# Six more block pairs of y in half products, Wv loaded behind them, and the residual of layer 0 on ScalarE and by an adding gather

## The chip, the cores and the metric

The kernel runs on one core of a Trainium2 chip, in fp32. The metric is device time in microseconds (us) of one launch, as the median of several runs. One further execution was taken with the hardware profiler; its views (busy times, windows, waits, timelines, the chain that ended last) are what this document argues from. TensorE is called PE in the views, VectorE DVE, ScalarE ACT, GpSimd POOL and the SyncE queue SP.

## The reference

Two layers on N = 2708 rows of D = 1024, over one sparse adjacency matrix. Cut to what matters:

```python
# layer 0
q = x @ Wq.T + bq;  k = x @ Wk.T + bk;  v = x @ Wv.T + bv
z = (q @ k.T) / sqrt(1024) * adj
z = where(z == 0, -10000, z)
x1 = layernorm(x + relu(softmax(z) @ v))
# layer 1
out = layernorm(x1 + adj @ (x1 @ W) + b)
```

## The kernel before, in words

**Blocks.** The rows are sorted by their number of neighbours and cut into 22 blocks of 128 (the last has 20). For a block, only the rows of x that its neighbours name are gathered.

**Algebra.** The scores q·k need only y = x·M with M = Wq·Wk (and some constants): a score is the dot product of a row of y with a row of x. Since softmax weights sum to one, the weighted sum is taken over rows of x first and projected by Wv afterwards. So layer 0 is: M, y for all blocks, scores, softmax and weighted row sums per block (`attend`), then a projection by Wv, relu, the residual and the layer norm.

**Stages.** From 0 to about 131 us TensorE makes M while VectorE lists the adjacency's columns. From 131 to 245 us it makes y for blocks 0 to 7, two blocks at a time, by `pair_products` (L334): Strassen-Winograd's scheme with seven half products of 8 passes (one pass is a 128x128 weight load and a 128x512 matmul) where two plain blocks take eight. From 245 to about 428 us it makes y for blocks 8 to 20, one after another, by `y_block` (L383, 32 passes), and the 20 rows of block 21 by `y_last` (L445). Then come ten projection pairs, again by `pair_products`, to about 745 us, and layer 1 to the end.

**pair_products.** It needs the four block sums S0 to S3 of the rows (made by GpSimd in `y_sums_of`, L402, for y; by VectorE for the projection) and three weight differences t2 to t4. Its three PSUM banks pa, pb and pc (`bank`, L321: four buffers in all) are used again inside the pair: product 3 (S1·t2) goes on in the bank of product 1, after its copy to SBUF; product 5 (S2·t3) in that of 3, after its copy; product 6 in that of 4, after its copy; product 7 in that of 5, after an add. The copies are `nc.scalar.copy` when there is no base to add (y), and VectorE adds when there is (the projection's bias); both are in `add` (L327, the instruction at L330 or L332). There are four ScalarE copies and three or more VectorE adds per pair of y.

**y_block.** A plain block fills two accumulators of 16 passes each; every third block takes its two banks from the transposes' pool (`spare_bank`, L324; "tr" in the views). ScalarE copies both to `yo` and SP stores it.

**Order of the work.** Each engine takes its instructions in the order in which the program was scheduled. The attention of the blocks is cut into jobs; a list of steps (y blocks, then projection pairs) hands them out by a credit: each step adds a planned time (`COST`, `STEP`, `PAIR`, ...) and each job takes its own off, so the constants decide how many jobs come between two steps. A job gathers rows (GpSimd, `gather_slot`, L482, and `gather_onto`, L472, where ScalarE first copies a row and the gather adds to it), takes dot products (VectorE, L1020), a softmax (ScalarE, L1058), and weighted sums (ScalarE L1077 for the first, VectorE L1079 for the others). ScalarE also sums x's columns (`column_sums`, L458, eight instructions a block).

**finish_pair** (L1214). After a projection, per half of a block, VectorE takes relu of t and adds the row of x, which GpSimd gathered ahead into a buffer (L1220, with the row sum as a by-product); then `norm` (ScalarE L982 and L995 with small VectorE steps) and a scatter of x1 (L926).

**Buffers.** Gathered rows go into G1 = 9 buffers, used in turn, in layer 1 too. Wv (16 loads of 256 KB) is loaded piecewise during y; the differences t3 and t4 of y's weights have a pool of their own.

Of the kernel before, what the change touches and what calls it, by code (L numbers as in the profile page):

```python
# [9 lines left out]
F32 = mybir.dt.float32  # L10
# [4 lines left out]
U8 = mybir.dt.uint8  # L15
# [26 lines left out]
EARLY = 13  # L42
G1 = 9
RB = 5
# [39 lines left out]
def sparse_part(ctx, tc, x, xT, adj, wqT, wkT, wvT, bq, bk, bv, w1, b1, out):  # L84
# [28 lines left out]
    with es:  # L113
# [219 lines left out]

        def pair_products(A, S, w, ts, base, to, whole, first_alone=False):  # L334
# [26 lines left out]
            add(to[0][1], pa, base[0][1])  # L361
            half_products(pc, S[0], t1, stop=False)
            add(to[1][1], pc, base[1][1])
            half_products(pa, S[2], t3, start=False, stop=False)
            whole(1, 1, pa, to[1][1])
            half_products(pc, S[3], w22, start=False)
            whole(0, 1, pc, to[0][1])
            products.append(half_products(pa, a22, t4, start=False))
            whole(1, 0, pa, base[1][0])
# [13 lines left out]
        def y_block(b):  # L383
            yo = yos[b % 3]
            to = halves_of(yo)
            firsts = []
            for h in range(NH):
                po = spare_bank() if b % 3 == 1 else bank()
                for c in range(DC):
                    put = nc.tensor.matmul(po, xts[b][:, c, :], m_q[c // 4][h][:, c % 4], start=(c == 0), stop=(c == DC - 1))  # L390
                    if c % (DC // 2) == 0:
                        firsts.append(put)
                add(to[h], po, None)
            products.append(put)
            if b != NB - 2:
                column_sums(b, firsts)
            if b == NB - 4:
                column_sums(NB - 2, [put] * (DC // 2))
            load_x()
            y_store(b, yo)  # L400

        def y_sums_of(b):  # L402
            (a11, a12), (a21, a22) = [halves_of_turned(x_) for x_ in xts[b:b + 2]]
            S = [y_sums[b // 2 % 2][:, i] for i in range(4)]
            nc.gpsimd.tensor_tensor(S[0], a21, a22, op=ALU.add)
            nc.gpsimd.tensor_tensor(S[1], S[0], a11, op=ALU.subtract)
            nc.gpsimd.tensor_tensor(S[3], a12, S[1], op=ALU.subtract)
            nc.gpsimd.tensor_tensor(S[2], a11, a21, op=ALU.subtract)

        def y_pair(b):  # L410
            yo = [yos[(b + k) % 3] for k in range(2)]
            to, base = [halves_of(t) for t in yo], [[None] * NH] * 2
            left = [NH, NH]

            def whole(k, h, acc, what):
                add(to[k][h], acc, what)
                left[k] -= 1
                if not left[k]:
                    load_x()
                    y_store(b + k, yo[k])  # L420

            at = len(began)
            pair_products(xts[b:b + 2], [y_sums[b // 2 % 2][:, i] for i in range(4)], y_w, y_t, base, to, whole)
            firsts = began[at:]
            for k in range(2):
                column_sums(b + k, firsts[3 * k:3 * k + 4])
            if b + 2 < FAMILY:
                y_sums_of(b + 2)
# [28 lines left out]

        def column_sums(b, behind=None):  # L458
            xt = xts[b] if b < NB - 1 else x_last
            for c in range(DC):  # L460
                put = nc.scalar.activation(junka[:, :xt.shape[2]], xt[:, c, :], AF.Copy, accum_out=xs[:, c, b:b + 1])  # L461
                if behind is not None and c % 2 == 0:
                    follow(put, behind[c // 2])
# [40 lines left out]
        def deal_hub():  # L504
# [71 lines left out]
            nc.tensor.matmul(mm[:, P:P + 1], ones, more, start=True, stop=True)  # L576
            place = small("place", P)
            nc.vector.tensor_copy(place, mm[:, :P])
# [231 lines left out]
        wb.release()  # L810
        yb = tc.alloc_tile_pool(name="yb", bufs=1, reuse_waits="tile")
        y_sums = []
        y_sums.append(yb.tile([P, 4, DC // 2, P], F32, name="y_s0"))
        t3 = yb.tile([P, DC // 2, HALF], F32, name="y_t3")
        t4 = yb.tile([P, DC // 2, HALF], F32, name="y_t4")
        y_sums.append(yb.tile([P, 4, DC // 2, P], F32, name="y_s1"))
# [4 lines left out]
        junka = xa.tile([P, P], F32, name="junka", bufs=1)  # L821
        x_last = xa.tile([P, DC, HUB], F32, name="x_last", bufs=1)
        nc.vector.memset(x_last, 0.0)
        xts = []
# [16 lines left out]

        def load_wv(cs):
            for c in cs:
                for h in range(NH):
                    put = nc.sync.dma_start(out=wv_q[c // 4][h][:, c % 4, :], in_=wvT[c * P:(c + 1) * P, h * HALF:(h + 1) * HALF])
                    follow(put, products[-2])

        wv_q = [None, quarters_of("wv", (1,))[0]]
        while counted[0] < done:
            count_columns(began[-1])  # L850
        for b in range(0, FAMILY, 2):
# [23 lines left out]
            if b in (0, 2, 6):  # L875
                next(deal)
            if b >= 4:
                load_wv(range(DC // 2 + b - 4, DC // 2 + b - 2))
        later_records = sort_end(1, products[-1])
        wv_q[0] = quarters_of("wv", (0,))[0]  # L880
        yb.release()
        la.release()
# [331 lines left out]
        def finish_pair(pair, ts):  # L1214
            for k, (b, t) in enumerate(zip(pair, ts)):
                ends = half_stats() if k and pair == pairs[-1] else None
                xr, sums = pair_x[b], [stat.tile([P, 1], F32, name=f"sm{h}", bufs=6) for h in range(NH)]
# [11 lines left out]

        STEP, Y_END, PAIR, EVICT, FLIP, END, SLOT, SMALL = 14.2, 4.8, 24.3, 7.5, 2.2, 3.3, 2.6, 1.5  # L1230
        got, xb_bc, xb_pools, pair_x = {}, [], [], {}
# [8 lines left out]
        steps += [("p", pairs[0]), ("mean", tuple(last))] + [("p", pair) for pair in pairs[1:]]  # L1240
        COST = {"p": PAIR - EVICT + FLIP, "mean": 5.6, NB - 1: 2.0}

# [94 lines left out]

        credit = 0
        turned = {}
# [9 lines left out]

        for i, (kind, b) in enumerate(steps):  # L1350
# [4 lines left out]
            credit += COST.get(kind, COST.get(b, STEP - Y_END))  # L1355
            step[0] = i
            join(i, 3 if left_y else 1)
            if kind == "y" and b == NB - 3:
                (q11, q12), (q21, q22) = wv_q
                follow(nc.vector.tensor_sub(q12, q12, q11), products[-2])  # L1360
            if kind == "p" and b == pairs[0]:

                wv_t = differences()
# [16 lines left out]
            if kind == "y":  # L1380
# [9 lines left out]
                if 3 <= b - FAMILY < 7:  # L1390
                    load_wv([b - FAMILY - 3])
                if b == FAMILY + 1:
                    column_sums(NB - 1)
                left_y -= 1
# [464 lines left out]
```

## Time and profile before

| what | us |
|---|---|
| median of three runs | 1039.84 |
| lowest, highest run | 1035.62, 1050.41 |
| the profiled execution's own time | 1041.33 |
| its span | 1039.6 |
| TensorE, VectorE, ScalarE, GpSimd busy | 966.2, 834.8, 424.5, 581.6 |
| mean granted TensorE clock | 0.971 of full |

In the lines below, a row of the waits is: engine, line and tile that waited, what it waited for, total us, times, longest us. A row of a timeline is: start, us, engine, line, operation, tiles and shapes, and in brackets the idle time before it with what ended it. A row of the groups is: line, engine, operation, tiles, count | busy us, mean ns of one | idle before. A row of the windows is: window, its length, then busy us (and instructions) of PE, PEld (weight loads), DVE, ACT and POOL, the granted clock, the DMA share and GB/s.

### The profile page before, as it was taken

Reading aid. Unit: us, or ns where it says so; the run is one execution under the profiler, and the core shown is the slowest. Engines: PE = TensorE matmul, PEld = TensorE weight load, DVE = VectorE, ACT = ScalarE, POOL = GpSimd, SP = SyncE. Lnnn points to the kernel's source line nnn. Section 1 sums busy time; section 2 is a strip of 40 time slices with the busy share of each in tenths; the row PEclk is TensorE's granted clock in tenths of the full one; section 3 lists DMA queues with packets and bytes.
Section 4 is the critical chain, followed back from the end, with each engine's and each line's share of the span. In section 5 each row is a group of like instructions: output and inputs, shape, how many; then the busy total and the mean of one; then the engine's idle time right before and its main releaser. Section 6 shows DMA issues by size and latency. Waiting matters only on the chain.

```text
span 1039.6 us, 10519 instructions
## 1 busy us (share of the span) xinstructions
PE 966.2 (93%) x2723; PEld 456.3 (44%) x2723; DVE 834.8 (80%) x2017; ACT 424.5 (41%) x932; POOL 581.6 (56%) x455
## 2 busy tenths in 40 slices
PE   7989987899999999897999999997899999989994
PEld 6434433344444444444544444443444444534441
DVE  8999997963768863999999999986569877869632
ACT  4634474554534434134343545322322333352721
POOL 3841044432666742456857776681678888868410
PEclk9989998999999999898999999998999999989997
DMA  9455896677889863345837888898598699987631
GB/s 353 150 185 172 240 288 188 191 251 192 211 257 316 274 199 113 120 125 153 247 109 214 265 237 248 270 277 318 173 306 215 218 298 309 310 261 220 186 116 44
DMA packets 103069, 229.23 MB, mean 220 GB/s; under 512 B 19678, under 2 KB 47078, under 8 KB 103000
## 3 DMA queue, kind: packets, MB, share of 16 engines
q0 software_dynamic: 51152, 159.06, 50.8%
q1 hardware_dynamic: 51848, 69.41, 20.8%
q8 instruction: 23, 0.38, 0.1%
q14 instruction: 46, 0.38, 0.1%
HBM read 218.10 MB, written 33.64 MB: 242 GB/s over the span
## 4 chain that ended last, share of the span: by engine, by line
PE 43%; DVE 24%; DMA 14%; issue 11%; POOL 5%; ACT 2%; SPq 0%; POOLq 0%; DVEq 0%; ACTq 0%
PE po L310 24%; PE po L390 11%; DVE at_a L239 6%; PE tr L390 5%; DMA g<-x_d,tabs 3%; POOL g L482 3%; DVE r L1455 2%; DVE junkv L1020 2%; DVE r L1079 1%; DMA xr<-x_d,tabs 1%; DMA yg<-y_d,tabs 1%; POOL xr L466 1%; DMA g<-in_x_dram,tabs 1%; DMA g<-x_d,tab_h 1%; DMA g<-in_x_dram,rec_h 1%
## 5 line engine op out<-in xcount | busy, mean ns | idle before, releaser
L310 PE MATMUL po<-t,s_all 128*128 128x512 f32 x320 | 146.5, 600 | 5.3 <-DVE xr L332 4.8
L482 POOL DMA_INDIRECT g<-in_x_dram,tabs x84 | 117.4, 1398 | 56.3 <-issue 14.6
L390 PE MATMUL po<-m,xt 128*128 128x512 f32 x288 | 124.8, 592 | 0.0
L1455 DVE SCALAR_TENSOR_TENSOR r<-g,valid,r 128x1024 f32<-128x1024 f32 x77 | 98.1, 1280 | 13.8 <-DMA g<-x_d,tabs 10.8
L1020 DVE SCALAR_TENSOR_TENSOR junkv<-yg,g 128x1024 uint8<-128x1024 f32 x84 | 102.4, 1219 | 4.4 <-DMA yg<-y_d,tabs 2.7
L310 PEld LDWEIGHTS po<-t,s_all 128*128 128x128 f32 x320 | 60.7, 192 | 83.3 <-issue 70.7
L482 POOL DMA_INDIRECT g<-x_d,tabs x66 | 78.3, 1186 | 23.2 <-issue 14.6
L1079 DVE SCALAR_TENSOR_TENSOR r<-g,pr,r 128x1024 f32<-128x1024 f32 x64 | 81.8, 1279 | 6.4 <-ACT r L1077 5.8
L390 PEld LDWEIGHTS po<-m,xt 128*128 128x128 f32 x288 | 54.6, 190 | 68.2 <-issue 67.7
L982 ACT ACTIVATE junks<-t,lnm 128x1024 uint8<-128x1024 f32 (+1 forms) x40 | 45.9, 1147 | 93.6 <-DVE lnm L980 93.5
L239 DVE FIND_INDEX8 at_a<-ones,a 128x8 uint16<-128x83 f32 (+3 forms) x132 | 82.0, 627 | 0.0
L310 PE MATMUL po<-wv,s_all 128*128 128x512 f32 x160 | 74.5, 610 | 8.0 <-DVE t L332 6.4
L310 PE MATMUL po<-w,rT 128*128 128x512 f32 x160 | 75.2, 612 | 4.4 <-DVE t L1492 4.2
L461 ACT ACTIVATE junka<-xt 128x128 f32<-128x128 f32 x168 | 51.8, 308 | 61.1 <-PE po L310 28.2
L255 ACT ACTIVATE junk<-a 128x2756 uint8<-128x2756 uint32 (+1 forms) x22 | 55.0, 2501 | 49.7 <-issue 31.6
L310 PE MATMUL po<-t,rT 128*128 128x512 f32 x160 | 74.4, 608 | 0.7 <-DVE t L332 0.7
L940 ACT COPY rT<-tr 128x512 f32<-128x512 f32 x76 | 41.3, 588 | 81.2 <-PE tr L939 81.1
L310 PE MATMUL po<-wv,rT 128*128 128x512 f32 x160 | 73.9, 613 | 0.0
L310 PE MATMUL po<-w,s_all 128*128 128x512 f32 x160 | 72.4, 593 | 0.7 <-DVE xr L332 0.7
L995 ACT ACTIVATE t<-t,nmr,rstd 128x1024 f32<-128x1024 f32 (+1 forms) x40 | 48.8, 1237 | 42.7 <-DVE nmr L994 38.2
L390 PE MATMUL tr<-m,xt 128*128 128x512 f32 x128 | 55.6, 592 | 0.0
L926 POOL DMA_INDIRECT x_d<-t,tabs x22 | 27.2, 1236 | 45.8 <-ACT t L995 35.1
(415 smaller groups left out, 1818.1 us busy)
## 6 DMA issues: line engine op xcount, KB each, us to landing
xt<-in_xT_dram SPq DMA_DIRECT2D x21, 512.0 KB, 8.9
y_d<-yo SPq DMA_DIRECT2D x21, 512.0 KB, 6.8
a<-in_adj_dram SPq DMA_DIRECT2D x21, 413.5 KB, 5.9
a<-in_adj_dram SPq DMA_DIRECT2D x21, 338.5 KB, 5.1
a<-in_adj_dram SPq DMA_DIRECT2D x21, 263.5 KB, 3.3
wq_i<-in_wqT_dram SPq DMA_DIRECT2D x8, 512.0 KB, 7.0
wk_i<-in_wkT_dram SPq DMA_DIRECT2D x8, 512.0 KB, 10.2
wv<-in_wvT_dram SPq DMA_DIRECT2D x16, 256.0 KB, 10.0
```

Source lines behind the costliest of these rows:

```text
L239: nc.vector.max_index(at[:n, i], ones[:n, :8], a[:n, cuts[i] + 8 * i:cuts[i + 1] + 8 * i + 8])
L255: put = nc.scalar.activation(junk[:n], loaded[b][:n, :AW].bitcast(U32), AF.Sign, accum_out=cnt[:n, b:b + 1])
L310: put = nc.tensor.matmul(acc, a[:, k], w[:, k], start=start and k == 0, stop=stop and k == DC // 2 - 1, skip_group_check=True)
L390: put = nc.tensor.matmul(po, xts[b][:, c, :], m_q[c // 4][h][:, c % 4], start=(c == 0), stop=(c == DC - 1))
L461: put = nc.scalar.activation(junka[:, :xt.shape[2]], xt[:, c, :], AF.Copy, accum_out=xs[:, c, b:b + 1])
L482: nc.gpsimd.indirect_dma_start(out=dst[:n], out_offset=None, in_=src, in_offset=bass.IndirectOffsetOnAxis(ap=at, axis=0), bounds_check=N - ...
L940: nc.scalar.copy(rT[:, g * 4:g * 4 + 4, :], tr)
L982: nc.scalar.activation(junks[:n], t[:n], AF.Square, bias=nm[:n], accum_out=vs[:n])
L995: applied.append(nc.scalar.activation(t[:n], t[:n], AF.Identity, bias=nmr[:n], scale=rstd[:n]))
L1020: put = nc.vector.scalar_tensor_tensor(junkv[:n], yg[:n], scale, xg[:n], op0=ALU.mult, op1=ALU.mult, accum_out=s)
L1079: nc.vector.scalar_tensor_tensor(r[:n], xg[j][:n], pr[:n, j:j + 1], r[:n], op0=ALU.mult, op1=ALU.add)
L1455: put = nc.vector.scalar_tensor_tensor(r[:n], xg[:n], ok[:n, j:j + 1], r[:n], op0=ALU.mult, op1=ALU.add)
```

## The change

**Pairs.** Blocks 8 to 19 of y are made as six pairs by `y_pair` instead of twelve plain blocks; block 20 stays plain, after block 21. The jobs of the second block of a pair are now placed behind product 4 (`halfway`). The block sums have one buffer each instead of two, and S2 is written over the first half of the second block's own rows; x's column sums of these columns are put right by a scale of 2 in the first block and −1 in the second. Plain blocks no longer use the transposes' banks.

**Wv.** t3 and t4 live in two of Wv's slots, and Wv is loaded whole behind the last pair.

**finish_pair.** For all projection pairs but the last, ScalarE takes relu of t in place, GpSimd gathers x's rows onto t by adding, and ScalarE takes the sum by a pass of its own. No buffer of x's rows is gathered ahead for these pairs.

**Constants.** G1 is 8 instead of 9; a half of a pair is planned at 8.9 us, and the end of a block at 2.0 instead of 3.3.

```diff
-G1 = 9
+G1 = 8
...
-            half_products(pc, S[0], t1, stop=False)
+            put = half_products(pc, S[0], t1, stop=False)
+            if halfway is not None:
+                products.append(put)
+                halfway()
...
         def y_sums_of(b):
             (a11, a12), (a21, a22) = [halves_of_turned(x_) for x_ in xts[b:b + 2]]
-            S = [y_sums[b // 2 % 2][:, i] for i in range(4)]
-            nc.gpsimd.tensor_tensor(S[0], a21, a22, op=ALU.add)
-            nc.gpsimd.tensor_tensor(S[1], S[0], a11, op=ALU.subtract)
-            nc.gpsimd.tensor_tensor(S[3], a12, S[1], op=ALU.subtract)
-            nc.gpsimd.tensor_tensor(S[2], a11, a21, op=ALU.subtract)
+            s0, s1, s3 = y_sums
+            nc.gpsimd.tensor_tensor(s0, a21, a22, op=ALU.add)
+            nc.gpsimd.tensor_tensor(s1, s0, a11, op=ALU.subtract)
+            nc.gpsimd.tensor_tensor(a21, a11, a21, op=ALU.subtract)
+            nc.gpsimd.tensor_tensor(s3, a12, s1, op=ALU.subtract)
...
+            def halfway():
+                column_sums(b, began[at:at + 4], 2.0)
+                load_x()
+                if ahead is not None:
+                    ahead()
+
+            s0, s1, s3 = y_sums
+            pair_products(xt, [s0, s1, xt[1][:, :DC // 2], s3], y_w, y_t, base, to, whole, halfway=halfway)
+            column_sums(b + 1, began[at + 3:at + 7], -1.0)
+            if b + 3 < NB - 1:
                 y_sums_of(b + 2)
...
+        t3, t4 = [wv_pool.tile([P, DC // 2, HALF], F32, name=f"y_t{k}", tag=f"v{k - 1}") for k in (3, 4)]
...
         def finish_pair(pair, ts):
             for k, (b, t) in enumerate(zip(pair, ts)):
-                ends = half_stats() if k and pair == pairs[-1] else None
+                if pair != pairs[-1]:
+                    nc.scalar.activation(t, t, AF.Relu)
+                    gather_at(x, tabs[:, b, ROW:ROW + 1], P, t, ALU.add)
+                    sm = stat.tile([P, 1], F32, name="sm")
+                    nc.scalar.activation(junks, t, AF.Copy, accum_out=sm)
+                    norm(t, sm, P)
+                    scatter(x1_d[:, :], b, P, t, "x1")
+                    continue
+                ends = half_stats() if k else None
...
-        STEP, Y_END, PAIR, EVICT, FLIP, END, SLOT, SMALL = 14.2, 4.8, 24.3, 7.5, 2.2, 3.3, 2.6, 1.5
+        STEP, Y_END, HALF_PAIR, PAIR, EVICT, FLIP, END, SLOT, SMALL = 14.2, 4.8, 8.9, 24.3, 7.5, 2.2, 2.0, 2.6, 1.5
...
-                (y_last if b == NB - 1 else y_block)(b)
...
+        for i, (kind, b) in enumerate(steps):
+            if kind != "y" or b >= NB - 2 or b % 2 == 0:
+                ahead(i)
+            if kind == "y":
+                if b < NB - 2:
+                    if b % 2 == 0:
+                        y_pair(b, lambda: ahead(i + 1))
...
+                        if b == NB - 4:
+                            column_sums(NB - 2, [products[-1]] * (DC // 2))
+                            wv_q = quarters_of("wv")
+                            load_wv()
+                else:
+                    (y_last if b == NB - 1 else y_block)(b)
...
-                for k, b_ in enumerate(b):
+                for k, b_ in enumerate(b if b == pairs[-1] else ()):
                     pair_x[b_] = gather_x(x, b_, k)
```

More of the change, by code (lines that the diff above doesn't have):

```diff
@@ L332, in add, with pair_products @@
                     nc.vector.tensor_add(to, acc, what)
-        def pair_products(A, S, w, ts, base, to, whole, first_alone=False):
+        def pair_products(A, S, w, ts, base, to, whole, first_alone=False, halfway=None):
             (w11, t1), (w21, w22) = w
@@ L385, in y_block @@
             to = halves_of(yo)
-            firsts = []
             for h in range(NH):
-                po = spare_bank() if b % 3 == 1 else bank()
+                po = bank()
                 for c in range(DC):
                     put = nc.tensor.matmul(po, xts[b][:, c, :], m_q[c // 4][h][:, c % 4], start=(c == 0), stop=(c == DC - 1))
-                    if c % (DC // 2) == 0:
-                        firsts.append(put)
                 add(to[h], po, None)
             products.append(put)
[L395 to L399, printed above, removed]
             y_store(b, yo)
@@ L403, in y_sums_of, with y_pair @@
             (a11, a12), (a21, a22) = [halves_of_turned(x_) for x_ in xts[b:b + 2]]
-            S = [y_sums[b // 2 % 2][:, i] for i in range(4)]
-            nc.gpsimd.tensor_tensor(S[0], a21, a22, op=ALU.add)
-            nc.gpsimd.tensor_tensor(S[1], S[0], a11, op=ALU.subtract)
-            nc.gpsimd.tensor_tensor(S[3], a12, S[1], op=ALU.subtract)
-            nc.gpsimd.tensor_tensor(S[2], a11, a21, op=ALU.subtract)
-        def y_pair(b):
+            s0, s1, s3 = y_sums
[3 more added lines that the diff above has]
+            nc.gpsimd.tensor_tensor(s3, a12, s1, op=ALU.subtract)
+        def y_pair(b, ahead=None):
             yo = [yos[(b + k) % 3] for k in range(2)]
@@ L418, in whole @@
                 if not left[k]:
-                    load_x()
+                    if k:
+                        load_x()
                     y_store(b + k, yo[k])
             at = len(began)
[L423 to L427, printed above, removed]
+            xt = xts[b:b + 2]
+            def halfway():
+                column_sums(b, began[at:at + 4], 2.0)
+                load_x()
+                if ahead is not None:
[4 more added lines that the diff above has]
+            if b + 3 < NB - 1:
                 y_sums_of(b + 2)
@@ L456, in y_last, with column_sums @@
                 nc.sync.dma_start(out=y_ds[1][o0:o0 + n, cs], in_=yo[gs, cs])
-        def column_sums(b, behind=None):
+        def column_sums(b, behind=None, of_first=1.0):
             xt = xts[b] if b < NB - 1 else x_last
             for c in range(DC):
-                put = nc.scalar.activation(junka[:, :xt.shape[2]], xt[:, c, :], AF.Copy, accum_out=xs[:, c, b:b + 1])
+                put = nc.scalar.activation(junka[:, :xt.shape[2]], xt[:, c, :], AF.Copy, scale=of_first if c < DC // 2 else 1.0,
+                                           accum_out=xs[:, c, b:b + 1])
                 if behind is not None and c % 2 == 0:
@@ L576, in deal_hub @@
             nc.tensor.matmul(mm[:, P:P + 1], ones, more, start=True, stop=True)
-            place = small("place", P)
+            place = alike
             nc.vector.tensor_copy(place, mm[:, :P])
@@ L810, in sparse_part @@
         wb.release()
[L811 to L816, printed above, removed]
+        t3, t4 = [wv_pool.tile([P, DC // 2, HALF], F32, name=f"y_t{k}", tag=f"v{k - 1}") for k in (3, 4)]
         nc.vector.tensor_sub(t3, t2, m_q[0][0])
@@ L820, in sparse_part @@
         xs = xa.tile([P, DC, NB], F32, name="xs", bufs=1)
-        junka = xa.tile([P, P], F32, name="junka", bufs=1)
+        junka = xa.tile([P, P], U8, name="junka", bufs=1)
         x_last = xa.tile([P, DC, HUB], F32, name="x_last", bufs=1)
+        y_sums = [xa.tile([P, DC // 2, P], F32, name=f"y_s{i}", bufs=1) for i in (0, 1, 3)]
         nc.vector.memset(x_last, 0.0)
@@ L840, in sparse_part, with load_wv @@
         deal = deal_hub()
[L842 to L848, printed above, removed]
+        def load_wv():
+            for i in range(2):
+                for j in range(2):
+                    for c in range(DC // 2):
+                        nc.sync.dma_start(out=wv_q[i][j][:, c, :],
+                                          in_=wvT[(i * DC // 2 + c) * P:(i * DC // 2 + c + 1) * P, j * HALF:(j + 1) * HALF])
         while counted[0] < done:
@@ L876, in sparse_part @@
                 next(deal)
-            if b >= 4:
-                load_wv(range(DC // 2 + b - 4, DC // 2 + b - 2))
         later_records = sort_end(1, products[-1])
-        wv_q[0] = quarters_of("wv", (0,))[0]
-        yb.release()
         la.release()
@@ L1240, in sparse_part @@
         steps += [("p", pairs[0]), ("mean", tuple(last))] + [("p", pair) for pair in pairs[1:]]
-        COST = {"p": PAIR - EVICT + FLIP, "mean": 5.6, NB - 1: 2.0}
+        COST = {"p": PAIR - EVICT + FLIP, "mean": 5.6, NB - 1: 2.0, NB - 2: STEP - Y_END}
         def blocks_of(step):
@@ L1336, in raise_flag @@
             nc.vector.tensor_scalar(flag, mm[:1, 0, :1], 0.0, None, op0=ALU.is_gt)
-        credit = 0
+        credit, wv_q = 0, None
         turned = {}
@@ L1348, in turn, with ahead @@
                             ring.remove(b_)
-        for i, (kind, b) in enumerate(steps):
+        def ahead(i):
+            nonlocal credit, pending, wv_t
+            kind, b = steps[i]
             for p in pending:
@@ L1354, in sparse_part @@
             pending = []
-            credit += COST.get(kind, COST.get(b, STEP - Y_END))
+            credit += COST.get(kind, COST.get(b, HALF_PAIR))
             step[0] = i
             join(i, 3 if left_y else 1)
-            if kind == "y" and b == NB - 3:
+            if kind == "y" and b == NB - 2:
                 (q11, q12), (q21, q22) = wv_q
@@ L1361, in sparse_part @@
             if kind == "p" and b == pairs[0]:
+                (q11, q12), (q21, q22) = wv_q
                 wv_t = differences()
@@ L1388, in sparse_part @@
                     nc.sync.dma_start(out=bias_bc, in_=bv.to_broadcast([P, D]))
-                (y_last if b == NB - 1 else y_block)(b)
[L1390 to L1393, printed above, removed]
+        wv_t = None
+        for i, (kind, b) in enumerate(steps):
[5 more added lines that the diff above has]
+                        y_pair(b, lambda: ahead(i + 1))
+                        if b == FAMILY:
+                            column_sums(NB - 1)
+                        if b == NB - 4:
[4 more added lines that the diff above has]
+                    (y_last if b == NB - 1 else y_block)(b)
                 left_y -= 1
```

## The prediction

> **What bounds the kernel now.** I read the page's busy times and chain first.
>
> ```profile
> PE 966.2 (93%) x2723; PEld 456.3 (44%) x2723; DVE 834.8 (80%) x2017; ACT 424.5 (41%) x932; POOL 581.6 (56%) x455
> PE 43%; DVE 24%; DMA 14%; issue 11%; POOL 5%; ACT 2%; SPq 0%; POOLq 0%; DVEq 0%; ACTq 0%
> ```
>
> TensorE leads and VectorE follows, but an average over stages says little. So next the busy time in the windows of the stages that the change touches (columns: window, length, then each engine's busy us).
>
> ```profile
> 165.00:245.00 80.00, 76.48 (x191) 34.68 (x190) 56.75 (x225) 42.62 (x124) 26.07 (x26) 1.00 0.67 213
> 245.00:413.00 168.00, 168.00 (x449) 74.62 (x448) 110.43 (x195) 75.73 (x287) 94.97 (x72) 1.00 0.77 227
> 540.00:600.00 60.00, 59.58 (x163) 27.85 (x162) 59.83 (x135) 27.58 (x54) 43.08 (x31) 1.00 0.79 231
> ```
>
> From 245 to 413 us (y, blocks 8 to 20) TensorE has no gap at all, VectorE is busy two thirds of the time and GpSimd 57%: a pure TensorE stage. From 428 to about 745 us (ten projection pairs) both TensorE and VectorE are near full.
>
> Third, the waits between 245 and 428 us (total, times, longest), and ScalarE's timeline in the middle of them:
>
> ```profile
> ACT yo L330 <- PE po L390: 26.7, 12, 6.3
> ACT pr L1058 <- DVE nms L1049: 11.2, 2, 9.3
> ACT pr L1058 <- DVE nm L1049: 9.2, 2, 7.7
> ACT yg L477 <- DVE junkv L1020: 6.2, 1, 6.2
> ACT xr L477 <- DVE junkv L1020: 5.1, 1, 5.1
> ACT r L1077 <- DVE pr L1064: 4.8, 2, 4.1
> ```
> ```profile
> 307.85 0.30 ACT L1058 ACTIVATE pr<-scores,nms 128x6 f32<-128x6 f32 x1 [9.30 <-DVE nms L1049]
> 308.84 1.15 ACT L1077 ACTIVATE r<-g,pr 128x1024 f32<-128x1024 f32 x1 [0.59 <-issue]
> 310.62 0.57 ACT L330 COPY yo<-po 128x512 f32<-128x512 f32 x1
> ```
>
> ScalarE, which empties y's PSUM banks, stands for up to 9.3 us at a softmax step whose scores VectorE has not finished. The copy of y behind it runs at 310.62, about ten microseconds after TensorE ended block 11 (near 299.9). TensorE lost nothing: a plain block has two finished accumulators and seven banks rotate.
>
> Last, the durations:
>
> ```profile
> L1220 DVE SCALAR_TENSOR_TENSOR t<-t,xr 128x512 f32<-128x512 f32 x40 | 26.8, 682 | 0.1
> L466 POOL DMA_INDIRECT xr<-x_d,tabs x22 | 38.6, 1752 | 13.6 <-ACT xr L1465 7.8 <-issue 4.0 <-DMA out_dram<-t,tabs 0.6
> L982 ACT ACTIVATE junks<-t,lnm 128x1024 uint8<-128x1024 f32 (+1 forms) x40 | 45.9, 1147 | 93.6 <-DVE lnm L980 93.5
> L332 DVE TENSOR_TENSOR yo<-po,yo 128x512 f32<-128x512 f32 x12 | 8.1, 676 | 12.5 <-PE po L310 11.7 <-issue 0.8
> L406 POOL TENSOR_TENSOR y_s<-y_s,xt 128x512 f32<-128x512 f32 x4 | 5.1, 1272 | 0.0
> ```
>
> **What the Trainium skill says.** "PSUM — Partial Sum Buffer", section "Engine vs sequencer instructions": the ScalarE, VectorE and GpSimd queues are strict FIFO. The trace agrees: the copy at 310.62 has its product ready for ten microseconds and runs only after the two softmax steps. "SBUF — State Buffer", section "Who interferes with whom": a VectorE instruction with two SBUF inputs contends with a GpSimd instruction that reads SBUF, and the one that comes second is blocked. The trace agrees: while GpSimd makes a block sum (185.67 us, 1.27 us), a VectorE multiply of two SBUF tiles (L245, 185.85 us) takes 1.16 us instead of 0.21. "DMA: Bandwidth & Descriptors", section "SWDGE vs HWDGE vs iDMA": adding in a DMA can only be issued from GpSimd. So the new gather stands in GpSimd's queue; layer 1 has the same form, 1.75 us each.
>
> **The change, part by part** (against the profiled execution: 1041.33 us, span 1039.6).
>
> (1) *Six pairs in place of twelve plain blocks.* A product of 8 passes takes 8 x 0.429 = 3.43 us; a pair has 7 and two plain blocks 8. TensorE loses 6 x 3.43 = 20.6 us, all on the path. VectorE gains 18 adds x 0.68 = 12 us, in a stage where it idles 58 us. GpSimd gains 24 sums x 1.27 = 30 us on 95 of 168, and each can hold up a score product (1.22 us, two SBUF inputs) or be held up by it. ScalarE's copies stay at four a pair and its column sums at their number; the scale of 2 or −1 in them costs nothing, as the instruction is the same. The sums now have one buffer: their last reading is product 4 of one pair for the first two, and product 3 of the next needs the second, five products or 17 us later; four sums take 5.1 us, so they are hidden unless GpSimd's queue runs over 12 us late.
>
> What takes the gain away is the order inside a pair. Product 3 writes the bank that ScalarE must have copied after product 1; 5 waits for the copy of 3; 6 for that of 4; 7 for a VectorE add. One product (3.43 us) lies between, the copy takes 0.58: slack 2.85 us, where a plain block had over ten. In the new instruction order softmax steps still stand before such copies in the first three pairs (blocks 8 to 13). The five longest ScalarE waits of before in that stretch, less the slack each time: 9.30 → 6.4, 7.67 → 4.8, 6.24 → 3.4, 5.08 → 2.2, 4.12 → 1.3; sum 18.1 us. Those waits themselves move: GpSimd's fifth score gather of block 4 is the 17th instruction behind the stage's first gather instead of the 10th, and four of those in front are sums. By the durations it goes out 42 us after the stage's start instead of 32.7: 9.3 us more. The first pair loses some 3.5 us to VectorE's queue before product 7. Stalls: 18.1 + 9.3 + 3.5 = 31, so the stage changes by −20.6 + 31 = about +10. From block 14 on VectorE is ahead of its jobs, and I expect no stalls. Bounds: −20.6 (ScalarE keeps up) and +25 (half as much again).
>
> (2) *The start of y.* In before the first two loads of x's turned rows go out at 120.0, and TensorE needs them at 131.5. In after all four stand on SP's queue behind adjacency loads that went out at 130.9 to 133.6, so TensorE begins some 11 us later. But the first pair then waited 8.54 us for VectorE anyway (add L332), and VectorE is full until 165. I take +5 (bounds 0 and +11).
>
> (3) *Wv behind the last pair.* Sixteen loads of 256 KB, 10.0 us median to land. Block 20 (13.73 us) and the turning of the first pair cover them; VectorE's subtractions for the weights (2.2 us each) wait for the first of them. Before also lost about 6 us of TensorE between 427.5 and 433.4. On SP's queue twelve of the sixteen stand in front of the store of y's block 18, and one of the last four, which wait for the last pair's end, in front of block 19's: whoever gathers those rows waits, but scores of these blocks are due well inside the projection stage. Cost 0; with the cover gone, 10.
>
> (4) *finish_pair for nine of ten pairs.* VectorE loses 36 x 0.68 = 24.6 us. ScalarE gains 36 operations of about 1.15 (row L982) and 18 accumulator reads of 0.19: 45 us in a stage where it idles over half. GpSimd's 18 gathers cost 1.75 instead of 1.34: +7 us; each now waits for the relu in GpSimd's queue, in front of the score gathers, where the old ones ran ahead. From a pair's end to its rows' scatter I count 24 us instead of 14 (relu 1.2, gather issue and landing about 7.7, sum 1.3), inside the 31 to 36 after which a pair's buffers come round. Counting VectorE work between the adds of successive pairs in the new order gives 247 us instead of 260; TensorE's floor of about 26 a pair allows 266.9 → 259.8. So −7 to −13; I take −10.
>
> (5) *Eight gather buffers instead of nine* in all stages. The DMA wait in layer 1's sums (L1455) is 10.8 us now; one buffer less is one landing (6.2) now and then. I take +1 (0 to +6).
>
> Sum: +10 + 5 + 0 − 10 + 1 = +6, so 1041.3 + 6 = 1047.3. The profiled execution lies 1.5 above the median of the three runs, 1039.84: forecast 1046.
>
> **Rivals.**
> B, *the pairs deliver*: ScalarE's softmax steps come early enough, stalls 4 us, start +2, projection −13: −20.6 + 4 + 2 − 13 = −27.6, so 1012. For it: VectorE has 58 us of idle in the stage. Against: VectorE's idle lies in its second half, the ScalarE waits in the first.
> C, *slower: GpSimd held by the added gathers*. Place: the projection stage. Before, a scatter that waited for ScalarE held GpSimd 4.4 us a time (35.1 us in 8 waits between 428 and 745). Eighteen gathers that wait for a relu at that price are 79 us, beside 115 us of idle of GpSimd there. Eight buffers hold 8 x 1.22 = 9.8 us of score work; a score gather takes 5.6 us to land, so from a hold of about 4.2 us on VectorE runs dry. If a third of the 79 is exposed: +26, so 1072.
> D, *Wv comes late*: its loads compete with stores and gathers, the cover is gone: +10, so 1056.
> That the change doesn't do what it says is no case: TensorE's instruction order has 48 matmuls fewer in y.
>
> **How the numbers follow.** Chances: A (the forecast) 0.42, B 0.32, C 0.18, D 0.08. A's own range is 1030 to 1062. The range reaches most of B and C: 1008 to 1071. Two per cent of 1039.84, about what a measurement can tell from no change, is 20.8: bounds 1019 and 1060.6. Faster: 0.27 of B. Same: 0.05 of B, 0.39 of A, 0.04 of D: 0.48. Slower: 0.18 of C, 0.03 of A, 0.04 of D: 0.25.
>
> **What would show it.** Step 1: waits of TensorE on "ACT yo L330" in the y stage, tens of microseconds in all, behind ScalarE waits on pr and r; pairs of blocks 8 to 13 at 30 us or more, those of 14 to 19 near 24. If all six take 24 to 26, B is right and the FIFO argument wrong. Step 2: TensorE's first y product near 142 instead of 131.5. Step 3: a gap of under 8 us before the first projection. Step 4: pairs of about 26 us, VectorE no longer full; long GpSimd waits on the relu with VectorE waiting for gathered rows would be C. Step 5: layer 1 as long as before, within 6 us. The forecast falls if score work runs far enough ahead that no softmax step is late, or if the first projection waits for Wv.

## The result and the profile after

The changed kernel takes 1111.91 us in the median (1105.77 to 1114.23) against 1041.16 us: ratio 1.0661, 95% interval [1.0571, 1.0751]. The forecast was 1046 with a range up to 1071, so it was wrong, and the loss lies where a gain of 10 us was expected.

Three points cut both profiles into stages: TensorE's first product of y, its first projection product, and its first product of layer 1.

| stage (us) | before | after | difference | forecast |
|---|---|---|---|---|
| up to y's first product | 131.5 | 141.2 | +9.7 | together with the next row +15 |
| y, up to the first projection | 301.9 | 301.5 | −0.4 | (see above) |
| ten projection pairs | 310.9 | 367.1 | +56.2 | −10 |
| layer 1 and end | 295.4 | 299.1 | +3.7 | +1 |

The page's busy times first (columns as before):

```profile
PE 971.9 (88%) x2675; PEld 454.6 (41%) x2675; DVE 850.5 (77%) x1963; ACT 460.0 (41%) x986; POOL 610.7 (55%) x479
PE 22%; issue 15%; DMA 15%; POOL 11%; DVE 10%; ACT 2%; POOLq 0%; DVEq 0%; ACTq 0%
```

With 48 matmuls fewer TensorE is shown busy as long as before (the granted clock is 0.942 instead of 0.971), and it carries only 22% of the chain instead of 43%, with 15% each of issue and DMA. The windows, at the same times as those of the kernel before in the prediction:

```profile
165.00:245.00 80.00, 71.16 (x160) 31.19 (x161) 58.36 (x182) 39.58 (x116) 36.74 (x36) 0.94 0.61 190
245.00:413.00 168.00, 153.23 (x393) 66.93 (x395) 129.25 (x223) 67.98 (x258) 116.22 (x86) 0.94 0.66 187
540.00:600.00 60.00, 52.14 (x155) 25.57 (x155) 50.64 (x106) 29.19 (x55) 33.20 (x24) 0.99 0.58 143
```

In the second, VectorE is busy 129 us instead of 110 and TensorE has gaps. In the third, a slice of the projection stage, no engine is full any more: VectorE went from 59.8 of 60 to 50.6, TensorE from 59.6 to 52.1. That points to a chain of waits, not a busy engine. The waits of this stage show where to look, first in the kernel before (433 to 744 us), then in the changed one (442 to 810 us); columns as before:

```profile
PE po L310 <- DVE t L332: 7.6, 3, 6.4
...
ACT junks L982 <- DVE lnm L980: 63.5, 16, 15.2
...
POOL x_d L926 <- ACT t L995: 35.1, 8, 9.7
```

```profile
ACT t L1213 <- DVE t L332: 56.8, 14, 17.0
ACT junks L1216 <- DMA t<-in_x_dram,tabs: 52.6, 14, 6.8
...
DVE lnm L974 <- ACT junks L1216: 38.7, 12, 6.2
...
PE po L310 <- DVE t L332: 31.9, 11, 7.8
...
POOL t L470 <- ACT t L1213: 21.2, 6, 7.7
```

L1213 is the new relu, L470 the adding gather, L1216 the new sum, L974 the first VectorE step of the norm. Long waits of ScalarE and GpSimd were there before too. New are VectorE's waits for the sum, and TensorE waits 31.9 us for VectorE's add instead of 7.6. One turn of it in ScalarE's timeline, and what VectorE did at the same time:

```profile
660.49 1.05 ACT L1213 ACTIVATE t<-t 128x1024 f32<-128x1024 f32 x1
662.42 1.08 ACT L936 COPY rT<-tr 128x512 f32<-128x512 f32 x2 [0.89 <-PE tr L935]
663.74 1.06 ACT L1213 ACTIVATE t<-t 128x1024 f32<-128x1024 f32 x1 [0.23 <-DVE t L332]
664.70 1.05 ACT L936 COPY rT<-tr 128x512 f32<-128x512 f32 x2
672.29 1.06 ACT L1216 ACTIVATE junks<-t 128x1024 uint8<-128x1024 f32 x1 [6.54 <-DMA t<-in_x_dram,tabs]
...
673.66 1.15 ACT L978 ACTIVATE junks<-t,lnm 128x1024 uint8<-128x1024 f32 x1 [0.22 <-DVE lnm L974]
```
```profile
673.47 0.15 DVE L974 TENSOR_SCALAR lnm<-sm 128x1 f32<-128x1 f32 x1 [4.89 <-ACT junks L1216]
```

The sum stands in ScalarE's queue until the rows have landed; VectorE's 0.15 us step for the mean waits for the sum, with score work behind it in VectorE's queue; the next pair's adds come late, and TensorE waits for them.

A wait of TensorE can cost more than its own length here. Eight passes of the same shape, just before a wait of 7.8 us and just after it:

```profile
770.70 3.60 PE L310 MATMUL po<-t,s_all 128*128 128x512 f32 x8
782.10 5.75 PE L310 MATMUL po<-wv,s_all 128*128 128x512 f32 x8 [7.80 <-DVE t L332]
```

The granted clock is 0.50 from 782 to 786 us and 1.00 again from 787. Over the whole stage nearly the same number of matmuls (874 and 872 in the two profiles) keeps TensorE busy for 303.7 us instead of 290.1. So of the 56 us some 43 are more idle time of TensorE and 13.6 are slower products.

The y stage is as forecast in kind. TensorE waits for ScalarE's copies, which stand behind softmax steps and weighted sums:

```profile
PE po L310 <- ACT yo L330: 12.9, 3, 4.6
```
```profile
294.23 1.15 ACT L1073 ACTIVATE r<-g,pr 128x1024 f32<-128x1024 f32 x1 [5.40 <-DVE pr L1060]
...
296.36 0.57 ACT L330 COPY yo<-po 128x512 f32<-128x512 f32 x1
...
324.97 0.30 ACT L1054 ACTIVATE pr<-scores,nms 128x6 f32<-128x6 f32 x1 [5.86 <-DVE nms L1045]
...
327.89 1.15 ACT L1073 ACTIVATE r<-g,pr 128x1024 f32<-128x1024 f32 x1 [1.80 <-DVE pr L1060]
328.94 0.57 ACT L330 COPY yo<-po 128x512 f32<-128x512 f32 x1
```

The first three pairs take 31.9, 32.9 and 31.6 us (starts at 253.47, 285.40, 318.32 and 349.90), the fourth and fifth 24.3 and 24.0. In the first three, TensorE's waits are 14.7 us in all, and the products right after the three waits of about 4 us take 8.5 us longer than elsewhere (8 passes 6.75 instead of 3.60, 16 passes 9.34 and 10.11 instead of 7.03).

### The profile page after: what moved, and what is told of

It is laid out like the page before. It is cut to its first block, busy times and chain, and to the rows that moved or that the text cites. A ratio compares the mean times of both kernels' runs of the same rounds, so it can differ in the third digit from the quotient of the medians.

```text
span 1108.9 us, 10460 instructions
## 1 busy us (share of the span) xinstructions
PE 971.9 (88%) x2675; PEld 454.6 (41%) x2675; DVE 850.5 (77%) x1963; ACT 460.0 (41%) x986; POOL 610.7 (55%) x479
## 3 DMA queue, kind: packets, MB, share of 16 engines
q1 hardware_dynamic: 51848, 69.41, 19.6%
## 4 chain that ended last, share of the span: by engine, by line
PE 22%; issue 15%; DMA 15%; POOL 11%; DVE 10%; ACT 2%; POOLq 0%; DVEq 0%; ACTq 0%
PE po L310 20%; DMA g<-in_x_dram,tabs 5%; POOL g L486 4%; DMA g<-x_d,tabs 3%; DMA t<-in_x_dram,tabs 2%; DVE junkv L1016 2%; POOL xr L470 2%; POOL g L470 2%; DMA yg<-y_d,tabs 1%; DVE r L1473 1%; DMA xr<-x_d,tabs 1%; DVE r L1152 1%; DMA y_d<-yo 1%; POOL t L470 1%; DVE t L332 1%
## 5 line engine op out<-in xcount | busy, mean ns | idle before, releaser
L310 PE MATMUL po<-t,s_all 128*128 128x512 f32 x320 | 150.5, 614 | 20.1 <-DVE t L332 15.5
L486 POOL DMA_INDIRECT g<-in_x_dram,tabs x84 | 109.3, 1302 | 74.2 <-ACT r L1073 26.3
L1016 DVE SCALAR_TENSOR_TENSOR junkv<-yg,g 128x1024 uint8<-128x1024 f32 x84 | 109.7, 1306 | 28.6 <-DMA yg<-y_d,tabs 14.9
L1075 DVE SCALAR_TENSOR_TENSOR r<-g,pr,r 128x1024 f32<-128x1024 f32 x64 | 85.1, 1330 | 6.4 <-ACT r L1073 5.7
L310 PE MATMUL po<-t,rT 128*128 128x512 f32 x160 | 78.9, 638 | 8.1 <-DVE t L332 7.5
L310 PE MATMUL po<-y_t,xt 128*128 128x512 f32 x160 | 74.7, 611 | 11.6 <-DVE yo L332 9.1
L310 PE MATMUL po<-y_t,y_s 128*128 128x512 f32 x160 | 76.1, 629 | 8.9 <-ACT yo L330 8.9
L464 ACT ACTIVATE junka<-xt 128x128 uint8<-128x128 f32 x168 | 51.8, 308 | 70.7 <-PE po L310 65.3
L310 PE MATMUL po<-m,xt 128*128 128x512 f32 x160 | 72.1, 604 | 7.5 <-DMA xt<-in_xT_dram 7.5
L978 ACT ACTIVATE junks<-t,lnm 128x1024 uint8<-128x1024 f32 (+1 forms) x40 | 45.8, 1146 | 40.5 <-DVE lnm L976 34.7
L935 PE MATMUL tr<-ident,r 128*128 128x128 f32 x304 | 41.4, 284 | 19.4 <-DVE r L1075 5.2
```

Of the source, the lines that this page charges most:

```text
L310: put = nc.tensor.matmul(acc, a[:, k], w[:, k], start=start and k == 0, stop=stop and k == DC // 2 - 1, skip_group_check=True)
L486: nc.gpsimd.indirect_dma_start(out=dst[:n], out_offset=None, in_=src, in_offset=bass.IndirectOffsetOnAxis(ap=at, axis=0), bounds_check=N - ...
L935: nc.tensor.transpose(tr[:, k, :], r[:, c * P:(c + 1) * P], ident)
L978: nc.scalar.activation(junks[:n], t[:n], AF.Square, bias=nm[:n], accum_out=vs[:n])
L1016: put = nc.vector.scalar_tensor_tensor(junkv[:n], yg[:n], scale, xg[:n], op0=ALU.mult, op1=ALU.mult, accum_out=s)
L1075: nc.vector.scalar_tensor_tensor(r[:n], xg[j][:n], pr[:n, j:j + 1], r[:n], op0=ALU.mult, op1=ALU.add)
```

## The experiments

Theory F: the new finish_pair makes the in-order queues stand, and that is the 56 us. Rival P: the pairs with what came along (new places of the jobs, eight buffers, Wv late) slow the projection stage. Each ratio below is to the kernel before on the same chip. The stage lengths are from one profiled execution of each run, cut as above; the y stage, which the changed kernel and runs 1 to 8 except run 2 have alike, lasts from 296.4 to 301.5 us in them, so a few microseconds between two runs tell little.

**1. The changed kernel with the old finish_pair.**

```diff
-                if pair != pairs[-1]:
-                    nc.scalar.activation(t, t, AF.Relu)
-                    gather_at(x, tabs[:, b, ROW:ROW + 1], P, t, ALU.add)
...
-                    continue
-                ends = half_stats() if k else None
+                ends = half_stats() if k and pair == pairs[-1] else None
...
-                for k, b_ in enumerate(b if b == pairs[-1] else ()):
+                for k, b_ in enumerate(b):
```

> The changed kernel with finish_pair as before (relu and residual on VectorE, x rows gathered ahead, END 3.3). Theory F (ScalarE and VectorE stand in their queues for the relu, the adding gather and the sum; this made the projection stage 56 us longer): the stage between the first projection and the first layer-1 product goes from 367 us back to about 311, the whole to about 1056. Rival P (the pairs, the jobs' new places or the eight gather buffers slow the projection stage): it stays above 350, the whole above 1095.

Measured 1062.49 us, ratio 1.0213 [1.0164, 1.0261]; the projection stage takes 327.0 us. So finish_pair is worth some 40 us of the stage, and the rest of the change 16 of it: F holds for the larger part, P for the smaller. (The planned END goes with finish_pair: 3.3 in this run, 2.0 in the next. Runs 7 and 8 keep 2.0 and are short all the same.)

**2. The kernel before with the new finish_pair alone.**

```diff
+                if pair != pairs[-1]:
+                    nc.scalar.activation(t, t, AF.Relu)
+                    gather_at(x, tabs[:, b, ROW:ROW + 1], P, t, ALU.add)
...
-                for k, b_ in enumerate(b):
+                for k, b_ in enumerate(b if b == pairs[-1] else ()):
```

> The kernel before with the new finish_pair alone (END 2.0, nine gather buffers, plain blocks of y). Theory F: 40 to 60 us slower than before, 1080 to 1100, all in the projection stage, with ScalarE waits on the relu and on the sum of some 50 us each. Rival P: no slower than before, about 1030 to 1040, as VectorE is relieved of 24.6 us.

Measured 1089.45 us, ratio 1.0452 [1.0396, 1.0507]; projection stage 355.6 us. Its waits in that stage are those of the changed kernel:

```profile
ACT junks L1220 <- DMA t<-in_x_dram,tabs: 57.0, 14, 7.4
ACT t L1217 <- DVE t L332: 48.3, 12, 9.7
```
```profile
DVE lnm L978 <- ACT junks L1220: 39.6, 12, 6.1
```

VectorE's busy time in the stage falls from 280.6 to 262.0 us, so the work was indeed taken off it; its idle time rises from 30 to 94. The stage is 45 us longer than before. The two parts add up: +2.1% and +4.5% against +6.6% together.

**3 and 4. The sum placed later; everything placed later.**

```diff
                     gather_at(x, tabs[:, b, ROW:ROW + 1], P, t, ALU.add)
-                    sm = stat.tile([P, 1], F32, name="sm")
-                    nc.scalar.activation(junks, t, AF.Copy, accum_out=sm)
-                    norm(t, sm, P)
-                    scatter(x1_d[:, :], b, P, t, "x1")
+                    rest.append((b, t))
                     continue
...
                 credit -= run_job()
+            finish_rest()
             if not left_y:
                 turn(i)
```

In the fourth run the relu and the gather stand at the place of `finish_rest()`, and `finish_rest()` opens the next step.

> The changed kernel with the sum, norm and scatter of a pair placed behind the step's jobs; relu and adding gather stay where they are. If the stand at the landing is what costs (ScalarE 52.6 us at the sum, VectorE 38.7 us at the mean): both rows nearly vanish and the whole falls by 30 to 45, to 1067 to 1082. If the stand at the relu (56.8 us) or GpSimd's queue is what costs: under 15 us are won, above 1095.

> As the run before, and the relu and the adding gather too are placed behind the step's jobs, the sum and norm at the start of the next step, when the rows have landed. Theory F: no engine stands any more, the projection stage takes 300 to 315 us, the whole 1045 to 1060. If the added work itself (ScalarE 45 us, GpSimd's longer gathers) is the cost: above 1085.

Measured 1103.03 us (ratio 1.0581 [1.0522, 1.0640]; projection stage 363.2) and 1091.54 us (1.0505 [1.0445, 1.0565]; 352.6). Both fall short. In the order in which the program was scheduled the sum came forward again (in the third run a relu at 595.44 is followed by a sum at 599.94, with nothing else on ScalarE between): ScalarE still stands 47.9 and 39.5 us for the landing, VectorE 23.2 and 12.7 us for the sum.

**5. The sum behind a dependence on TensorE, and 6. relu on VectorE as well.**

```diff
-                nc.scalar.activation(junks, t, AF.Copy, accum_out=sm)
+                follow(nc.scalar.activation(junks, t, AF.Copy, accum_out=sm), behind)
...
+                at = len(began)
                 pending = [(finish_pair, b, project_pair(b, *turned[b]))]
+                finish_rest(began[at + 2])
```
```diff
-                    nc.scalar.activation(t, t, AF.Relu)
+                    nc.vector.tensor_scalar_max(t, t, 0.0)
```

> The changed kernel, with each pair's sum, norm and scatter put behind the third half product of the next pair by a dependence, so that the rows have landed (the placing alone, two runs ago, left most of the stand in place: 47.9 us at the sum and 23.2 at the mean). If the stand for the landing is the main part of the 40 to 45 us that finish_pair costs: both rows fall under 10 us and the whole to 1072 to 1082. If it is the relu or GpSimd's queue: under 15 us are won, 1095 or more.

> As the run before, and relu is taken on VectorE in place (18 operations more on VectorE), so that ScalarE stands at no relu and the adding gather waits for VectorE alone. If the stand at the relu (55 us in 11 to 14 waits of ScalarE) holds up others: 15 to 25 us under the run before, 1050 to 1062. If ScalarE's stand there is idle time that nobody waits for: equal to the run before or up to 12 us slower, by VectorE's added work.

Measured 1087.60 us (ratio 1.0435 [1.0390, 1.0481]; projection stage 355.9) and 1100.31 us (1.0557 [1.0510, 1.0603]; 363.3). In the fifth run the stand that I took for the cost is nearly gone, and the stage is still 356 us long in the profile:

```profile
DVE junkv L1291 <- DMA g<-in_x_dram,tabs: 19.5, 6, 6.4
DVE junkv L1016 <- DMA g<-in_x_dram,tabs: 17.9, 9, 3.7
...
DVE lnm L974 <- ACT junks L1236: 5.4, 2, 4.7
```
```profile
POOL x_d L922 <- ACT t L991: 42.6, 8, 16.9
```

VectorE waits 5.4 us at the mean instead of 38.7, but 37 us in two rows for gathered rows (22 in the changed kernel). GpSimd stands at the scatter of x1, which waits for the late norm, up to 16.9 us at a time, with the score gathers behind it; in the changed kernel that row has 37.6 us in all and 10.0 at the longest. So part of the stand may have moved on to the next queue in the chain; this is argued, not shown. The profile is also of run 5's slowest execution, 7.3 us above its median. By the ratios the run wins some 24 us against the changed kernel (1.0435 against 1.0661), so putting the sum later did help. The sixth run speaks against a loss by ScalarE's 57 us at the relu: without that wait the stage is 7 us longer, beside 12.5 us (18 operations) of added work on VectorE. But ScalarE stood 40.5 us for the landing again in that run, so it is no clean answer; runs 7 and 8 give one.

**7. Without the adding gather, and 8. with a gather that nobody waits for.** Both leave out layer 0's residual for nine of ten pairs.

```diff
-                    gather_at(x, tabs[:, b, ROW:ROW + 1], P, t, ALU.add)
```
```diff
-                    nc.scalar.activation(t, t, AF.Relu)
-                    gather_at(x, tabs[:, b, ROW:ROW + 1], P, t, ALU.add)
+                    put = nc.scalar.activation(t, t, AF.Relu)
+                    xr = (xb_pools[0] if k else wp).tile([P, D], F32, name="xr", bufs=2)
+                    gather_at(x, tabs[:, b, ROW:ROW + 1], P, xr, behind=put)
```

> The changed kernel without the adding gather (layer 0's residual is left out, for nine of ten pairs): relu, sum and norm stay on ScalarE, one after another. If the gather's place in the chain is the cost (its landing, and what it does to GpSimd's queue): the projection stage falls from 367 to 315 to 330 us, the whole to 1055 to 1072. If ScalarE's part alone is (relu that waits for VectorE, the longer way to the mean): it stays above 345, the whole above 1085.

> The changed kernel, with the gather of x's rows behind the relu as it is, but plain and into a buffer of its own that nobody reads (the residual is left out for nine of ten pairs): the sum and the norm do not wait for it. GpSimd's queue and the DMA traffic are as in the changed kernel, the chain relu to norm is as in the run without a gather (1071, projection stage 329.8 us). If GpSimd's queue is the cost: the stage stays at 350 or more, the whole above 1090. If the landing in the chain is: 325 to 340 us, the whole 1067 to 1082.

Measured 1071.22 us (ratio 1.0255 [1.0207, 1.0302]; stage 329.8) and 1072.15 us (1.0299 [1.0261, 1.0337]; stage 336.3). These two decide. With relu and sum on ScalarE but no transfer between them the stage is nearly as short as with the old finish_pair (327.0). With the transfer back in GpSimd's queue, behind the relu, but off the chain to the norm, it stays short. TensorE's waits for VectorE's add fall from 31.9 us to 9.8 and 12.6. ScalarE's wait at the relu is there in both (64.3 and 62.0 us instead of 56.8), so it costs nothing that shows; in run 8:

```profile
ACT t L1213 <- DVE t L332: 62.0, 11, 17.0
```

So 31 us (367.1 − 336.3) of the 40 come from the landing standing between relu and norm, and about 6.5 (336.3 − 329.8) from GpSimd's queue and the traffic. (Of the 31, TensorE's idle time is 20 and slower products are 10.6: it is busy 293.1 us in run 8, against 303.7.) The gather in run 8 is plain, not adding, and its issue takes 1.18 us instead of 1.75, so what the adding form costs more counts with the landing. The hold at the relu is also smaller in run 8: GpSimd waits 12.2 us for it, against 21.2 in the changed kernel. GpSimd's stand at the scatter does no harm by itself: in run 7 it is 34.2 us, nearly as in the changed kernel (37.6).

The two runs show one thing more. VectorE is busy 19.6 us less in this stage than in run 1 (273.3 and 273.2 us instead of 292.9), and the stage is no shorter: the relief that the forecast built on bought nothing that shows, even with the landing out of the way.

**9. The first loads of x on GpSimd's queue.**

```diff
-            nc.sync.dma_start(out=xt, in_=xT[:, r0:r0 + n].rearrange("(c p) n -> p c n", p=P))
+            (nc.gpsimd if b < 4 else nc.sync).dma_start(out=xt, in_=xT[:, r0:r0 + n].rearrange("(c p) n -> p c n", p=P))
```

> The changed kernel with the first four loads of x's turned rows issued by GpSimd instead of SP, so that they stand behind no adjacency load. If the late start of y (141.2 instead of 131.5) is carried to the end: 5 to 9 us faster, 1103 to 1107. If VectorE makes the first pairs wait anyway: no change beyond 3 us, the first pair only waits longer at product 7.

Measured 1108.04 us, ratio 1.0637 [1.0588, 1.0685]: the interval covers the changed kernel's 1.0661. In the profile y begins at 132.4 instead of 141.2, but the first pair then waits 8.31 us and the second 6.13 for VectorE's add, and block 8 begins at 250.8 instead of 253.5. So most of the late start was covered, as argued.

**10 to 12. What the six pairs of y are worth.** All three have the old finish_pair, so they stand against run 1 (1062.49 us, ratio 1.0213). Run 10 leaves out GpSimd's block sums for blocks 8 to 19; all matmuls still run. In run 11 VectorE makes the copies of the first three pairs. In run 12 blocks 8 to 13 are plain again, and the first loads of x are on GpSimd's queue as in run 9.

```diff
-            if b + 3 < NB - 1:
+            if b + 2 < FAMILY:
                 y_sums_of(b + 2)
```
```diff
-                if what is None:
+                if what is None and on_vector[0]:
+                    nc.vector.tensor_copy(to, acc)
+                elif what is None:
                     nc.scalar.copy(to, acc)
```
```diff
-            if kind != "y" or b >= NB - 2 or b % 2 == 0:
+            if kind != "y" or b >= NB - 2 or b % 2 == 0 or b < LATE:
                 ahead(i)
             if kind == "y":
-                if b < NB - 2:
+                if b < LATE:
+                    y_block(b)
...
+                elif b < NB - 2:
```

> The changed kernel with finish_pair as before, and without GpSimd's block sums for blocks 8 to 19 (20 of them left out, so that these blocks of y are wrong; all matmuls run). If the sums cost by the shared read port and by their place in GpSimd's queue: VectorE's score and sum products in the y stage come down from 1.39 to 1.56 us each to 1.22 to 1.29, 8 to 10 us of VectorE time, and the whole falls by 8 to 20 us, to 1042 to 1054. If they are hidden: 1059 to 1065.

> The changed kernel with finish_pair as before, and the four copies a pair of y that ScalarE makes taken by VectorE for blocks 8 to 13 (12 copies). If ScalarE's queue is what holds the first three pairs: TensorE's waits on ScalarE's copies (three of 3.6 to 4.1 us) vanish, the three pairs take 24 to 29 us each instead of 31.6, 33.2 and 30.1, and y ends 5 to 10 us earlier. If VectorE's progress is what sets the pace of all: those waits go over to VectorE, and the whole stays within 5 us of 1062.5 or gets slower by the 8 us of added copies.

> finish_pair as before, plain blocks 8 to 13 as before (banks of the transposes' pool too), pairs for blocks 14 to 19 alone, 9.4 us of jobs planned for a half pair, the first four loads of x on GpSimd. If the stalls of the first three pairs (31.9, 32.9 and 31.6 us, 14 us more than plain blocks) are what the pairs lose: y ends 15 to 20 us earlier than with all pairs and the old finish_pair (1062.5), the whole at 1035 to 1048. If blocks 14 to 19 gain nothing either, or the projection stage takes the gain back: above 1050.

Run 10: 1057.73 us, ratio 1.0126 [1.0084, 1.0169], some 9 us less than run 1 by the ratios. VectorE's score products in the y stage, in the run with the old finish_pair and then without the sums (busy us, mean ns of one, idle before):

```profile
L1016 DVE SCALAR_TENSOR_TENSOR junkv<-xr,g 128x1024 uint8<-128x1024 f32 x20 | 31.2, 1562 | 8.8 <-DMA g<-in_x_dram,tabs 6.3 <-DMA g<-in_x_dram,tab_h 2.5
```
```profile
L1016 DVE SCALAR_TENSOR_TENSOR junkv<-xr,g 128x1024 uint8<-128x1024 f32 x21 | 25.6, 1219 | 10.5 <-DMA g<-in_x_dram,tabs 7.5 <-DMA g<-in_x_dram,tab_h 3.0
```

VectorE's busy time in y falls from 228.3 to 209.4 us, but y gets only 5.5 us shorter (296.6 to 291.1).

Run 11: 1069.21 us, ratio 1.0236 [1.0181, 1.0292], in the whole not to be told from run 1. In the profile y takes 304.5 us instead of 296.6. TensorE's waits on ScalarE are gone and stand at VectorE, one of 7.38 us; the first three pairs take 31.7, 34.4 and 33.7 us (31.6, 33.2 and 30.1 in run 1). Whichever engine copies, the pairs wait.

Run 12: 1061.77 us, ratio 1.0181 [1.0124, 1.0238]. No gain that shows. Blocks 8 to 13 take 82.5 us, as in the kernel before, and then the first of the late pairs waits 8.75 us for ScalarE's copy and the second 6.09 us for VectorE's add; y takes 320.7 us, the projection stage 309.8. In this run more jobs are planned for a half pair (9.4 us instead of 8.9), and what the projection stage gained, y lost: 630.5 us for both, against 623.6 in run 1 and 612.7 before. As y begins 8.1 us earlier than in run 1, layer 1 begins at nearly the same time, 762.9 us instead of 764.0.

## Why the prediction was wrong, step by step

**Part (4), finish_pair, failed: −10 forecast, +40 to +45 measured (runs 1 and 2).** VectorE was relieved as counted in kind (its busy time in the stage fell by 18.6 us in run 2, 24.6 counted over nine pairs), and the durations came out (relu and sum 1.06 us, gather 1.75). The failing sentence is "From a pair's end to its rows' scatter I count 24 us instead of 14 …, inside the 31 to 36 after which a pair's buffers come round". It asks only when the buffers come free, and so puts the cost of the landing at nothing. It does not ask who stands in line meanwhile. The runs show 31 us for the landing between relu and norm (run 8). The trace shows the sum waiting for the landing at the head of ScalarE's queue, and the mean waiting for the sum at the head of VectorE's, which was nearly full in the kernel before. That the 31 us pass just this way is argued: run 5 took the wait at the mean from 38.7 to 5.4 us and won only part of them. In the kernel before the rows were gathered ahead, and L1220 stood 0.1 us in all. For y I had shown how a copy stands in its queue behind the wait of another step; I did not apply it here. The gain of 10 was a second error: it took VectorE's work for what sets the pace of a pair, and runs 7 and 8 have that work 19.6 us shorter without a shorter stage.

**Rival C named the right place, with the wrong mechanism and too small a size.** It put 26 us on GpSimd, held by gathers that wait for the relu. Run 8 keeps part of that hold and costs about 6.5 us more in the stage than run 7; the landing costs 31.

**Part (1), the pairs: +10 forecast, about +1 measured** (188.5 us from block 8 to the first projection before, 189.2 after), with a loss of 24 us in the first three pairs (96.4 − 3 x 24.03) where I had 31, and a shorter handover. That 24 is near 31 is partly luck: only 14.7 of it are waits, and 8.5 are the slower products after them, which had no term. The waits on "ACT yo L330" are there as forecast, behind softmax steps, but they are 12.9 us and not tens. And the place where TensorE waits is not the cause: with the copies on VectorE (run 11) or pairs for the later blocks alone (run 12) the loss stays. That VectorE's score work sets the pace of this stretch is likely, but not shown. The pairs add 12 us of adds to it, and GpSimd's sums hold it up by 17 us in this stage of the changed kernel: 26 products at 1499 instead of 1227 ns, 20 at 1562 instead of 1222, 31 at 1385 instead of 1285. That is what "SBUF — State Buffer", section "Who interferes with whom", in the Trainium skill says of two SBUF inputs beside a GpSimd instruction that reads SBUF; run 10 agrees, 1219 ns with the sums gone. I named this contention and gave it no term in the sum. Run 10 also gives its worth: 18.9 us less of VectorE's time, but 5.5 us in y and some 9 us in the whole.

**The remaining +16 us in the projection stage of run 1 had no term.** VectorE is busy 12.3 us longer there (634 instructions instead of 614), as some jobs moved there from y; its idle time is 34 us against 30. That the planned 8.9 us per half pair shifts them is likely from run 12 (280.9 us busy, stage 309.8), but that run changes other things too, so it isn't shown.

**Part (2)**: first product +9.7 (forecast 11), of which 8.6 were left at block 8 (forecast 5); run 9 gets back 4 us in the whole, within the noise. **Part (3)**: no gap at the first projection beyond what was there before, as forecast. **Part (5)**: layer 1 takes 293.7 us with eight buffers in run 1 against 295.4 before, so no cost of the buffers shows. Run 2 has nine buffers and the new finish_pair, and takes 301.5; the cause of the changed kernel's +3.7 stays open.

Rival B (the pairs deliver, 1012) and D (Wv late) did not happen. No version tried here beats the kernel before.

## What to carry to other kernels

Before moving a step into a DMA, find the next instruction that needs its landing, and read who is queued behind it on that engine, then on the next engine in the chain: a tiny step (here 0.15 us for a mean) at the head of a full queue can hold up all that stands behind it. Pushing the waiting step later helped only in part here (run 5); taking the landing out of the chain did help, and the old finish_pair does so by gathering the rows ahead. To learn what a landing costs, keep the transfer and let nobody wait for it (run 8), beside a run without it (run 7). Work taken off an engine and passes saved on TensorE are not yet time won: 19.6 us of VectorE's work and 20.6 us of TensorE's passes were saved here, and neither stage became shorter. And a wait of TensorE is to be counted with the slower products that may follow it.

## What was not expected of the hardware

Both sides pay when GpSimd's block sums run beside VectorE's products: the sums took 1.41 us in the mean (L401, whole kernel) instead of 1.27, while the products of VectorE went up by as much as 340 ns each (1222 to 1562).

After some waits TensorE was granted half its clock for 4 to 6 us: the clock reads 0.50 from 275 to 281, from 297 to 301 and from 782 to 786 us in the changed kernel, after waits of 4.0, 4.6 and 7.8 us. The length of the wait alone does not decide it: eight passes took 5.37 us after a wait of 2.36 us (656.58 us, changed kernel) and 3.70 us after one of 3.05 us (190.11 us, kernel before). What does decide it stays open.
